# Graph attention with residual and norm: 35 more tiles of x kept in DRAM, and another order in the lead-in

## The chip, the cores and the metric

The kernel runs on one core of one Trainium2 chip. The metric is the device time of one execution in microseconds (us). TensorE (PE), VectorE (DVE), ScalarE (ACT) and GpSimd (POOL) compute; SyncE (SP), ACT and POOL issue DMA transfers. PEld stands for TensorE's loads of weights.

## The reference

For 16 graphs x of 1024 nodes with 512 features, all with the same 0/1 matrix adj of 1024 x 1024, attention with 8 heads of 64 is computed in which a node attends to its neighbours alone; a residual and a layer norm follow.

```python
q = x @ Wq + bq;  k = x @ Wk + bk;  v = x @ Wv + bv        # 8 heads of 64
scores = q . k / sqrt(64) + (1 - adj) * -1e9
out = softmax(scores) @ v @ Wo + bo
x = layernorm(x + out)                                      # over the 512 features, eps 1e-5
```

The inputs have few edges: the probability of an edge falls with both node numbers, so most nodes have at most eight neighbours and a few have many.

## The kernel before, in words

**Sparse attention by lists.** Nodes are ranked by their number of neighbours and put into eight tiles of 128, t = 0 to 7 (ADJ, `most`, `ranks`). A node of tile t has OWN[t] neighbours of its own (2, 1, 2, 3, 4, 5, 5, 7). What is above that in tiles 6 and 7 is spread over BLOCKS[t] further blocks (1 and 5), and a product with a 0/1 matrix, `sums`, adds these up. The lists of tiles 6 and 7 are made by `edges(6)` and `edges(7)`, two generators that search rows of adj (DVE maxima), place the result by a product with `before` (`poff`), write place marks (the lines at L677 to L688), multiply once more (`pe`), read out the keys (L702 to L714) and transpose the marks into `sums` (`pof`, copied by ACT).

**Blocks and steps.** For each batch b and tile t, a block is one neighbour for each of 128 nodes: POOL gathers 128 rows of k and v (`kvg`, L1260), DVE multiplies with q (`qk`, L1281) and sums by head (`s`, L1285), ACT takes the exponential and weighs v (`pv`, L1309), DVE adds up (L1325). There are 530 blocks. The program is written out by one loop over steps n, one block a step, with 39 steps ahead of block 0 (n = -39 to -1), the lead-in. Within a step, functions planned earlier by `later` run, then matmuls by an account of credit (`share`), then one piece of each generator in `preps` up to its next `yield`. Gathers run eight blocks ahead, products four steps ahead. The order on each engine is the order of the program; the engines wait for each other by semaphores.

**Dense work.** `fronts` is a list of matmul units for all batches: transpositions of x (`pxT`), then pairs of row tiles: q by plain products (`pq`), k and v by a Strassen-like form with seven products (`x`, `pp` for p4, p6 and p7, and `z`), evacuated by DVE and ACT (`e`, `w`, `g`, `kv`). Rows of q, k and v go to DRAM by SP. `finish` multiplies by Wo (`po`), and `complete` adds residual and bias and normalises; POOL scatters the rows to the output. Most PSUM results take one of four buffers with the tag "fill" (`fill_psum`); `x`, `z` and `sum` have their own.

**x for the residual.** x is gathered by rank twice by POOL: once for the dense work (`gather_x`, L1001) and once for the residual (`load_y`, L1029), unless the tile's number 8 b + t is in STORED. A stored tile is written by SP to `residual` out of its transposition step and read back by SP (L1026). The x tiles have three buffers; the gather that follows in the same buffer comes two steps later for a stored tile:

```python
if b * NT + t in STORED:
    nc.sync.dma_start(residual[b * NT + t], xs)
    later(2, lambda: load_x(n // NT, n % NT))
else:
    load_x(n // NT, n % NT)
```

**The lead-in around the change.** `edges(7)` starts at step -24 and `edges(6)` at -9 (REST_FROM). `bias_setup` starts at -8 (BIAS_AT): a broadcast of bk, norms of bk and bq (L399 to L405), transpositions of the biases (`pb`, L408 and L409), copies (L411 to L415, the last makes `bvb`), a product with Wo (`pb3`, L419; the trace calls both pb) and its addition to `bo_bc` (L421). `more_ranks` computes `shifts` and `others` at -7 and -6 on DVE (L552 to L578).

Of the kernel before, what the change touches and what calls it, by code (L numbers as in the profile page):

```python
# [10 lines left out]
F32 = mybir.dt.float32  # L11
# [20 lines left out]
KG_BUFS, Q_BUFS, QT_BUFS, PV_BUFS, Y_BUFS = 8, 5, 3, 5, 6  # L32
# [10 lines left out]
LAZY = 2  # L43

SPILL = (*(8 * b + t for b in range(4, 12) for t in (3, 6)), 102, 103, 106, 107)
STORED = {*SPILL, *(i for i in range(102, 128) if i % 8 > 1)}
LATE = 12

AHEAD_LAST = 11
# [24 lines left out]
P = 128  # L74
# [103 lines left out]
def kernel(  # L178
# [36 lines left out]
    nc = tc.nc  # L215
    B, N, D = x.shape
    HD = D // HEADS
    NPAIR = D // P
# [20 lines left out]
    ident = const.tile([P, P], F32, name="ident")  # L239
# [4 lines left out]
    bias_qk = const.tile([P, 2 * NPAIR], F32, name="bias_qk")  # L244
# [3 lines left out]
    def broadcast(t, v):  # L248
        nc.scalar.dma_start(t, bass.AP(tensor=v.tensor, offset=v.offset, ap=[[0, P], [1, D]]))
# [4 lines left out]
    with ExitStack() as main:  # L254
        one = main.enter_context(tc.tile_pool(name="one", bufs=1))
        work = main.enter_context(tc.tile_pool(name="work", bufs=1))
# [4 lines left out]
        def fill_psum(name):  # L261
            return psum.tile([P, HALF], F32, tag="fill", name=name, bufs=4)
# [80 lines left out]
        def number(b, t):  # L343
            return b * NT + t if t < NT else -1
# [4 lines left out]
        spill = {i: dram.tile([P, D], F32, name=f"spill_{i}") for i in SPILL}  # L349
        residual = {i: dram.tile([P, D], F32, name=f"residual_{i}") for i in sorted(STORED)}  # L350
        zeros = work.tile([P, D + HEADS], F32, tag="pv0", name="zeros", bufs=3)
        nc.gpsimd.memset(zeros, 0.0)
        bias_rows = work.tile([2 * NPAIR, D + HEADS], F32, tag="pv0", name="bias_rows", bufs=3)[:, 0:P]
        bv_rows = work.tile([NPAIR, D + HEADS], F32, tag="pv0", name="bv_rows", bufs=3)[:, 0:P]
# [37 lines left out]
            nc.scalar.dma_start(bv_rows, bv.rearrange("(c p) -> c p", p=P))  # L392

        def bias_setup():
            bk_bc = work.tile([P, D], F32, tag="y", name="bk_bc", bufs=Y_BUFS)
            broadcast(bk_bc, bk)
            yield
            n4 = small.tile([P, NPAIR], F32, name="bk_norms", bufs=1)
            nc.vector.tensor_tensor(bk_bc, bk_bc, bk_bc, op=OP.mult)  # L399
            nc.vector.tensor_reduce(n4, bk_bc.rearrange("p (h d) -> p h d", d=P), axis=AX.X, op=OP.add)  # L400
            nc.vector.tensor_reduce(bk_norm, n4, axis=AX.X, op=OP.max)
            n8 = small.tile([P, HEADS], F32, name="bq_norms", bufs=1)
            nc.vector.tensor_tensor(bk_bc, bq_bc, bq_bc, op=OP.mult)
            nc.vector.tensor_reduce(n8, bk_bc.rearrange("p (h d) -> p h d", d=HD), axis=AX.X, op=OP.add)
            nc.vector.tensor_reduce(bq_norm, n8, axis=AX.X, op=OP.max)  # L405
            yield
            pb = fill_psum("pb")
            nc.tensor.transpose(pb[:, 0:2 * NPAIR], bias_rows, ident[:2 * NPAIR, :2 * NPAIR])  # L408
            nc.tensor.transpose(pb[:, 2 * NPAIR:3 * NPAIR], bv_rows, ident[:NPAIR, :NPAIR])  # L409
            yield  # L410
            nc.vector.tensor_copy(bias_qk, pb[:, 0:2 * NPAIR])  # L411
            bv_col = one.tile([P, NPAIR], F32, name="bv_col")
            nc.vector.tensor_copy(bv_col, pb[:, 2 * NPAIR:3 * NPAIR])
            bvb = work.tile([P, NPAIR, P], F32, tag="y", name="bvb", bufs=Y_BUFS)
            nc.vector.tensor_copy(bvb, bv_col[:, :, None].to_broadcast([P, NPAIR, P]))  # L415
            yield
            pb = fill_psum("pb3")
            for c in range(NPAIR):
                nc.tensor.matmul(pb, bvb[:, c, :], W["o"][:, c, :], start=(c == 0), stop=(c == NPAIR - 1))  # L419
            yield  # L420
            nc.vector.tensor_tensor(bo_bc, pb, bo_bc, op=OP.add)  # L421
# [209 lines left out]
        def edges(t):  # L631
            nb, J, K = BLOCKS[t], DEGREE[t], OWN[t]
            tag, bufs = ("kvg", KG_BUFS) if J > 16 else ("kv", 5)
# [36 lines left out]
                nc.vector.tensor_tensor(check[:, 2 * NT + 1:2 * NT + 2], ranked[:, t, 1:2], st[:, 0:1], op=OP.subtract)  # L670

            nc.vector.tensor_scalar(deg, ranked[:, t, 1:2], -float(K), 0.0, op0=OP.add, op1=OP.max)
            yield
            po = fill_psum(f"poff_{t}")
            nc.tensor.matmul(po[:, 0:1], before, deg, start=True, stop=True)
            yield
            nc.vector.tensor_copy(off, po[:, 0:1])  # L677
            nc.vector.tensor_scalar(kl[:, J:J + 1], po[:, 0:1], -float(K), None, op0=OP.add)
# [7 lines left out]
            o, span = of, place[:, 0:nb * P]  # L686
            nc.vector.tensor_scalar(o, span, off, None, op0=OP.is_gt)
            nc.vector.scalar_tensor_tensor(o, span, end, o, op0=OP.is_le, op1=OP.mult)  # L688
            yield
            step = min(nb, HALF // (J + 3))  # L690
            assert step * J <= D
            for i0 in range(0, nb, step):
# [50 lines left out]
        def transpose_x(b, t):  # L743
            def pe():
# [5 lines left out]
                def out():  # L750
# [3 lines left out]
                    if t == 0 and b >= PAIRED_FROM:  # L754
# [7 lines left out]
                        nc.scalar.activation(sq[0:LONE, :], xs[0:LONE, :], AF.Square, accum_out=x_norm[0:LONE, b:b + 1])  # L762
                    if b * NT + t in STORED:
                        nc.sync.dma_start(residual[b * NT + t], xs)
# [251 lines left out]
        def load_y(b, t, k=None):  # L1016
# [7 lines left out]
            loaded[b, t] = now[0]  # L1024
            if number(b, t) in STORED:
                nc.sync.dma_start(Y[b, t], residual[b * NT + t])  # L1026
# [445 lines left out]
        for t, n in REST_FROM.items():  # L1472
            prep.setdefault(n, []).append(edges(t))
        prep.setdefault(BIAS_AT, []).append(bias_setup())
        prep.setdefault(CHECKS_AT, []).append(checks())
        preps = [loads(), ranks()]
# [146 lines left out]
```

## Time and profile before

| what | value |
|---|---|
| median of 3 runs | 1878.04 us (1875.33 to 1880.48) |
| profiled execution | 1888.5 us |
| its span, first to last instruction | 1886.7 us |
| mean granted TensorE clock | 0.988 |
| busy: PE, DVE, ACT, POOL | 1814.2, 1687.8, 1565.7, 1264.1 us |
| DMA | 544.64 MB, mean 289 GB/s |
| gathers of y by POOL | 93, mean 1096 ns each |
| stores and loads of `residual` by SP | 36 and 36, 256 KB each |

The profile is one execution; its rows are compared with its own span. Busy times of different engines overlap. In rows that show operations, an arrow points from what is read to what is written, with buffer numbers left out; a wait is given as engine, line, and what ended it.

### The profile page before, as it was taken

The page shows a single profiled execution, that of the slowest core. Times are in us where ns is not written, and L with a number is a line of the kernel's source. Part 1 is how long each engine was busy: PE and PEld are TensorE (multiplying, and loading weights), DVE is VectorE, ACT ScalarE, POOL GpSimd, SP SyncE. Part 2 cuts the span into 40 slices and gives each one's busy share as a digit, 9 for nine tenths or more (in the row PEclk, how much of TensorE's full clock was granted, in tenths as well). Part 3 has the DMA queues.
Part 4 walks back from the last instruction along what each step waited for, and adds up shares of the span by engine and source line. Part 5 has one row for each costly group of instructions (what it writes and reads, how often), then busy time and mean ns, then how long its engine had stood idle before and what let it go on. Part 6 is the DMA issues. An engine that isn't in the chain of part 4 may idle for free.

```text
span 1886.7 us, 25241 instructions
## 1 busy us (share of the span) xinstructions
PE 1814.2 (96%) x5136; PEld 878.0 (47%) x5150; DVE 1687.8 (89%) x3462; ACT 1565.7 (83%) x6184; POOL 1264.1 (67%) x1189
## 2 busy tenths in 40 slices
PE   7979999999999999999999999999999999999995
PEld 3434444454444444444444444444544444444442
DVE  6888788999988999999899999999999999997885
ACT  3627768988888897999889898999799999987785
POOL 1366665777675776767676776677767767665784
PEclk9989999999999999999999999999999999999997
DMA  7356687898888898998898988888988999899982
GB/s 280 115 167 213 214 271 244 281 338 294 310 278 268 288 315 308 310 319 305 286 310 304 328 291 322 312 297 319 316 322 306 312 352 337 297 329 316 350 312 110
DMA packets 188150, 544.64 MB, mean 289 GB/s; under 512 B 32602, under 2 KB 32622, under 8 KB 187986
## 3 DMA queue, kind: packets, MB, share of 16 engines
q0 software_dynamic: 116400, 382.82, 60.5%
q1 hardware_dynamic: 68510, 154.30, 22.0%
q10 hardware_dynamic: 3076, 5.82, 0.9%
q14 instruction: 121, 0.99, 0.2%
q8 instruction: 43, 0.70, 0.1%
HBM read 419.52 MB, written 144.34 MB: 299 GB/s over the span
## 4 chain that ended last, share of the span: by engine, by line
PE 64%; DVE 12%; ACT 9%; issue 5%; DMA 2%; POOL 2%; SPq 0%; another core or an unknown queue 0%; POOLq 0%; DVEq 0%; ACTq 0%
PE po L790 16%; PE pq L790 13%; PE pp L947 11%; PE x L947 8%; PE z L947 8%; ACT pv L1309 6%; PE poT L1369 2%; DVE qk L1281 2%; PE pxT L748 2%; DVE s L1285 2%; PE sum L1335 2%; PE sum L1334 2%; ACT sq_k L800 1%; DVE pv L1325 1%; POOL kvg L1260 1%
## 5 line engine op out<-in xcount | busy, mean ns | idle before, releaser
L1309 ACT ACTIVATE pv<-kvg,pv 128x64 f32<-128x64 f32 x3600 | 908.3, 342 | 0.9 <-issue 0.7
L1260 POOL DMA_INDIRECT kvg<-kv_pair,place_row x462 | 521.7, 1129 | 261.5 <-issue 89.6
L790 PE MATMUL po<-wo,oT 128*128 128x512 f32 x816 | 374.4, 596 | 0.8 <-DVE g L966 0.3
L790 PE MATMUL pq<-wq,xT 128*128 128x512 f32 x792 | 368.7, 596 | 1.3 <-DVE q L821 0.9
L1285 DVE TENSOR_REDUCE s<-qk 128x8 f32<-128x512 f32 x530 | 360.5, 680 | 6.7
L1281 DVE TENSOR_TENSOR qk<-qt,kvg 128x512 f32<-128x512 f32 x434 | 296.7, 684 | 0.0
L947 PE MATMUL x<-b,xT 128*128 128x512 f32 x504 | 238.9, 596 | 0.5 <-issue 0.4
L947 PE MATMUL pp<-t,s 128*128 128x512 f32 x504 | 237.2, 593 | 1.6 <-DVE t L383 1.6
L790 PEld LDWEIGHTS po<-wo,oT 128*128 128x128 f32 x816 | 154.1, 191 | 176.2 <-issue 167.0
L1325 DVE TENSOR_TENSOR pv<-pv,pv 128x520 f32<-128x520 f32 x329 | 228.5, 694 | 4.5 <-ACT pv L1309 2.6
L790 PEld LDWEIGHTS pq<-wq,xT 128*128 128x128 f32 x792 | 148.0, 191 | 165.7 <-issue 154.2
L1001 POOL DMA_INDIRECT x<-in_x_dram,asked_row x120 | 130.3, 1086 | 85.2 <-PE pxT L748 34.6
L1125 POOL DMA_INDIRECT out_dram<-y,asked_row x129 | 148.3, 1150 | 39.2 <-issue 25.1
L1296 ACT ACTIVATE pv<-s,absent 128x8 f32<-128x8 f32 x434 | 127.5, 295 | 49.6 <-DVE s L1285 38.6
L800 ACT ACTIVATE sq_k<-kv 128x128 bf16<-128x128 f32 x512 | 151.1, 302 | 12.0 <-ACT sq_k L800 3.9
L947 PEld LDWEIGHTS x<-b,xT 128*128 128x128 f32 x504 | 94.8, 192 | 109.4 <-issue 102.0
L947 PEld LDWEIGHTS pp<-t,s 128*128 128x128 f32 x504 | 94.0, 190 | 109.3 <-issue 101.3
L1214 POOL DMA_INDIRECT qg<-q_rows,query_row x96 | 109.9, 1145 | 27.9 <-issue 25.2
L947 PE MATMUL z<-b,s 128*128 128x512 f32 x252 | 121.9, 607 | 4.3 <-DVE kv L975 3.3
L1029 POOL DMA_INDIRECT y<-in_x_dram,asked_row x93 | 102.0, 1096 | 35.8 <-issue 26.8
L947 PE MATMUL pp<-t,xT 128*128 128x512 f32 x252 | 120.4, 601 | 4.6 <-ACT mean L862 4.1
L1121 ACT ACTIVATE y<-y,stats 128x512 f32<-128x512 f32 (+1 forms) x129 | 103.8, 807 | 17.9 <-DVE stats L1116 14.4
(276 smaller groups left out, 2759.6 us busy)
## 6 DMA issues: line engine op xcount, KB each, us to landing
kv_pair<-kv SPq DMA_DIRECT2D x98, 512.0 KB
q_rows<-q SPq DMA_DIRECT2D x106, 256.0 KB
qt<-q_rows SPq DMA_DIRECT2D x98, 256.0 KB
residual<-x SPq DMA_DIRECT2D x36, 256.0 KB
y<-residual SPq DMA_DIRECT2D x36, 256.0 KB
kv_rows<-kv SPq DMA_DIRECT2D x15, 512.0 KB
kvg<-kv_pair,place_row POOLq DMA_INDIRECT x462
kv_pair<-kv SPq DMA_DIRECT2D x28, 256.0 KB
```

The source lines that it names most:

```text
L790: nc.tensor.matmul(p, lhs(c), w[:, c, :], start=(c == 0), stop=(c == NPAIR - 1))
L800: nc.scalar.activation(sq, s[:, ts(h, P)], AF.Square, scale=scale, accum_out=sums[:, h:h + 1])
L947: nc.tensor.matmul(R[bank], l[:, ts(c, P)], right[:, c, :], start=(first and c == 0), stop=(c == 1), skip_group_check=True,)
L1001: nc.gpsimd.indirect_dma_start(out=y, out_offset=None, in_=x_rows, in_offset=bass.IndirectOffsetOnAxis(ap=asked_row[:, t:t + 1], axis=0), ...
L1125: nc.gpsimd.indirect_dma_start(out=out_rows[b, t], out_offset=bass.IndirectOffsetOnAxis(ap=rows, axis=0), in_=y, in_offset=None, element_o ...
L1214: nc.gpsimd.indirect_dma_start(out=q, out_offset=None, in_=q_rows[b % ROWS], in_offset=bass.IndirectOffsetOnAxis(ap=rows, axis=0))
L1260: nc.gpsimd.indirect_dma_start(out=KG[n], out_offset=None, in_=rows, in_offset=bass.IndirectOffsetOnAxis(ap=(place_row if b else key_row)[ ...
L1281: nc.vector.tensor_tensor(QK[n], q, KG[n][:, 0:D], op=OP.mult)
L1285: nc.vector.tensor_reduce(S[n], QK.pop(n).rearrange("p (h d) -> p h d", d=HD), axis=AX.X, op=OP.add)
L1296: nc.scalar.activation(PV[n][:, D:], S.pop(n), AF.Exp, bias=bias)
L1309: nc.scalar.activation(pv[:, ts(h, HD)], v[:, ds(D + h * HD, HD)], AF.Copy, scale=pv[:, D + h:D + h + 1])
L1325: nc.vector.tensor_tensor(PV[b, t], PV[b, t], pv, op=OP.add)
```

## The change

Three edits are made. First, STORED takes in the tiles with numbers from 10 to 101 whose t is 2, 5 or 7: 35 tiles, 71 in all. Second, in `bias_setup` the transpositions of the biases come first, their copies one step later and ahead of the norms, and the product with Wo comes four yields behind the norms. Third, in `edges` there are four yields instead of one ahead of the first product, two instead of one behind it, and three instead of one behind the place marks.

```diff
-STORED = {*SPILL, *(i for i in range(102, 128) if i % 8 > 1)}
+STORED = {*SPILL, *(i for i in range(10, 102) if i % 8 in (2, 5, 7)), *(i for i in range(102, 128) if i % 8 > 1)}
...
         def bias_setup():
+            pb = fill_psum("pb")
+            nc.tensor.transpose(pb[:, 0:2 * NPAIR], bias_rows, ident[:2 * NPAIR, :2 * NPAIR])
+            nc.tensor.transpose(pb[:, 2 * NPAIR:3 * NPAIR], bv_rows, ident[:NPAIR, :NPAIR])
             bk_bc = work.tile([P, D], F32, tag="y", name="bk_bc", bufs=Y_BUFS)
             broadcast(bk_bc, bk)
+            yield
+            nc.vector.tensor_copy(bias_qk, pb[:, 0:2 * NPAIR])
+            bv_col = one.tile([P, NPAIR], F32, name="bv_col")
+            nc.vector.tensor_copy(bv_col, pb[:, 2 * NPAIR:3 * NPAIR])
+            bvb = work.tile([P, NPAIR, P], F32, tag="y", name="bvb", bufs=Y_BUFS)
+            nc.vector.tensor_copy(bvb, bv_col[:, :, None].to_broadcast([P, NPAIR, P]))
             yield
             n4 = small.tile([P, NPAIR], F32, name="bk_norms", bufs=1)
...
             nc.vector.tensor_reduce(bq_norm, n8, axis=AX.X, op=OP.max)
-            yield
-            pb = fill_psum("pb")
-            nc.tensor.transpose(pb[:, 0:2 * NPAIR], bias_rows, ident[:2 * NPAIR, :2 * NPAIR])
-            nc.tensor.transpose(pb[:, 2 * NPAIR:3 * NPAIR], bv_rows, ident[:NPAIR, :NPAIR])
-            yield
-            nc.vector.tensor_copy(bias_qk, pb[:, 0:2 * NPAIR])
-            bv_col = one.tile([P, NPAIR], F32, name="bv_col")
-            nc.vector.tensor_copy(bv_col, pb[:, 2 * NPAIR:3 * NPAIR])
-            bvb = work.tile([P, NPAIR, P], F32, tag="y", name="bvb", bufs=Y_BUFS)
-            nc.vector.tensor_copy(bvb, bv_col[:, :, None].to_broadcast([P, NPAIR, P]))
-            yield
+            for _ in range(4):
+                yield
             pb = fill_psum("pb3")
...
             nc.vector.tensor_scalar(deg, ranked[:, t, 1:2], -float(K), 0.0, op0=OP.add, op1=OP.max)
-            yield
+            for _ in range(4):
+                yield
             po = fill_psum(f"poff_{t}")
             nc.tensor.matmul(po[:, 0:1], before, deg, start=True, stop=True)
             yield
+            yield
             nc.vector.tensor_copy(off, po[:, 0:1])
...
             nc.vector.scalar_tensor_tensor(o, span, end, o, op0=OP.is_le, op1=OP.mult)
-            yield
+            for _ in range(3):
+                yield
             step = min(nb, HALF // (J + 3))
```

## The prediction

> **What bounds the kernel now.** I read the busy shares and the slices of the page first, then the windows by stage, then TensorE's waits, then the instructions in order of time where it waits.
>
> ```profile
> PE 1814.2 (96%) x5136; PEld 878.0 (47%) x5150; DVE 1687.8 (89%) x3462; ACT 1565.7 (83%) x6184; POOL 1264.1 (67%) x1189
> ...
> PE   7979999999999999999999999999999999999995
> ...
> q0 software_dynamic: 116400, 382.82, 60.5%
> q1 hardware_dynamic: 68510, 154.30, 22.0%
> ```
>
> TensorE (PE) is busy for all but 72.5 us of the span (1886.7 - 1814.2). The low slices stand at both ends. By the windows, PE is busy 1430.5 of the 1450 us from 250 to 1700: 19.5 us of idle. Up to 250 us it idles 27.1 us, and 10.1 from 50 us on are in this window:
>
> ```profile
> 100.00:150.00 50.00, 38.94 (x104) 17.44 (x103) 38.66 (x112) 15.12 (x62) 28.87 (x27) 0.86 0.57 181
> 150.00:200.00 50.00, 49.86 (x144) 23.90 (x143) 42.32 (x85) 40.15 (x172) 33.58 (x32) 1.00 0.66 211
> ```
>
> The columns are the stretch, then busy us of PE, PEld, DVE, ACT and POOL, granted clock, DMA share, GB/s. TensorE's waits there are two (us in total, times, longest):
>
> ```profile
> PE pb L419 <- DVE bv_col L413: 8.9, 1, 8.9
> PE poff L675 <- DVE check L670: 2.1, 1, 2.1
> ```
>
> These are the instructions around the first (start, us, what, idle before):
>
> ```profile
> 127.12 1.88 PE L790 MATMUL pq<-wq,xT 128*128 128x512 f32 x4
> 137.94 6.43 PE L419 MATMUL pb<-wo,bvb 128*128 128x512 f32 x8 [8.94 <-DVE bv_col L413]
> ...
> 152.40 3.60 PE L790 MATMUL pq<-wq,xT 128*128 128x512 f32 x8
> ```
>
> The bias product (pb3 in the code, pb in the trace) waits 8.94 us for a copy that VectorE (DVE) reaches late, and its eight matmuls then take 6.43 us where eight others take 3.60: 2.8 us more at a low clock. The prize is 8.9 + 2.8 = 11.7 us. DVE in the same place:
>
> ```profile
> 115.82 0.69 DVE L966 TENSOR_TENSOR g<-pp,w 128x512 f32<-128x512 f32 x1 [2.71 <-PE pp L947]
> ...
> 137.27 0.15 DVE L413 COPY bv_col<-pb 128x4 f32<-128x4 f32 x1
> ...
> 139.12 0.68 DVE L963 TENSOR_TENSOR w<-pp,e 128x512 f32<-128x512 f32 x1
> ...
> 146.47 0.68 DVE L821 SCALAR_TENSOR_TENSOR q<-pq,bq_bc 128x512 f32<-128x512 f32 x1
> ```
>
> From 117 to 142 DVE has no gap but short ones between its own dependent instructions. So here two engines are near their limit: PE waits for one copy, but behind that copy DVE is full.
>
> **What the Trainium skill says.** "TensorE: Matmul & The Clock Gate", Part 1, has the array fall to half clock after some 3.4 us idle and come back after as long a busy stretch; the 6.43 against 3.60 us agrees. The same page's table calls VectorE's queue strictly in order, so a copy emitted behind other work waits for all of it: that is the stall above. "DMA: Bandwidth & Descriptors", Issuing engines are not separate DMA queues: transfers of SP and of GpSimd (POOL) share 16 DMA engines, so a move from one to the other saves issue time and no transfer; the two queue rows agree in that both draw on one share. The same page's Anatomy of one DMA prices a transfer at 2.0 us + bytes/436 GB/s, 2.6 us for 256 KB as an estimate; the trace has no landing times for it, but its longest wait for such a store, 3.1 us, is near.
>
> **Part 1: 35 tiles kept.** Tiles 10 to 101 with t of 2, 5, 7: 33 in batches 1 to 11 and two in batch 12. Each adds a store of x and a load of y on SP (70 issues at the 0.41 us of the present rows, 29 us on an engine that mostly waits), and takes a gather of y from POOL: 35 x (1.10 + 0.30 issue) = 49 us of POOL. 35 gathers of x come two steps later (some 7 us; a step is about 3.3 us, 1737 us over 530 steps). They are used about 8 steps on (60 pairs over some 520 steps), so no transposition comes to wait.
>
> DMA: 70 x 256 KB = 18.4 MB more on q1 at 22.0/154.3 % per MB is +2.6 % of the span; 9.2 MB fewer on q0 at 60.5/382.8 is -1.5 %. The share goes up by 1.2 points, from 0.90 to about 0.92 in the middle. It is 0.95 at 1450 to 1500 us and PE is busy for all 50.0 us there.
>
> What could that change on the path? TensorE's longest waits from 250 to 1700 us:
>
> ```profile
> PE pm L858 <- DVE vsum L854: 3.8, 3, 1.9
> PE z L947 <- DVE kv L975: 3.3, 1, 3.3
> PE poT L1369 <- DVE o L1355: 3.0, 1, 3.0
> ```
>
> and POOL's for the stores of today:
>
> ```profile
> POOL x L1001 <- DMA residual<-x: 7.4, 5, 3.1
> ```
>
> No row names POOL or a transfer, so POOL's 49 us are hidden behind PE and gain nothing on the path. A gather of x that waits for its store holds the gathers of keys behind it in POOL's queue, for which DVE would wait; at 7.4/36 us each that is 7 us in all, at the longest each time 35 x 3.1 = 108. DVE waited for one such gather for 2.7 us in the whole stretch, so their lead of up to eight steps covers the first and probably most of the second. On SP a load of y waits for an older output store (13.7 us in 4 of 36 cases); the k, v and q stores and loads of query tiles queue behind it, and have steps to spare. I take 0, between -4 (a fifth of the 19.5 us idle) and +6 (a few late gathers).
>
> **Part 2: the lead-in.** Step numbers follow from the starts in the code; the trace has the same order. TensorE's instructions for list 7 move from steps -12, -10, -9 and -8 to -9, -4, -3 and -2 (a product, five products, four transpositions and one); DVE's nine small ones for its places (L677 to L688, 2.1 us) from -11 to -7 and nine behind the second product (L702 to L714, 3.0 us) from -9 to -3. ACT's two copies of sums go six steps later too. List 6's go from -3, -2, -1, 0 to 0, 2, 5, 6. The two bias transpositions go from -6 to -8, the three copies (0.6 us) from -5 to -7, the norms (3.0 us) from -7 to -6, the product from -4 to -2 and the addition from -3 to -1. The broadcast of bk stays at its step on ACT's queue.
>
> The 2.1 us wait of poff goes, and is worth nothing: the next thing on PE is the product of means at 109.66, which starts as DVE ends its sums at 109.6. From there I count on.
>
> PE: the second pp product of the pair (p7) ends at 115.7 as before, then z, p4, the second z and x, p6 and half of pq without the lists' products: 127.2. List 7's product, the other half of pq, the next x and the list's transpositions: 132.2. Then p7 of the next pair needs one of the four PSUM buffers "fill". They hold p6 (freed by w on DVE), pq (by q), and list 7's two results. Today the slot of p6 is free at 139.8 and nobody waits, since PE itself stands until 137.9.
>
> DVE: it loses the work that filled its gaps. It now idles from 111 to 115.8 and, behind g, from 116.4 to 118.5 for z. Then: second z, sums for the next pair and p4, to 121.2; places of list 7, to 123.2; shifts (2.1), to 125.3; copies, 125.9; one evacuation and the chain of others (L569 to L578, 4.7), 131.3; codes of list 6 (1.1), 132.4; norms, 135.5; sum and maxima (3.1), 138.5; first qk and s (1.3), 139.8; w to 140.4. So p7 starts at 140.4 and PE has stood for 8.2 us: **the stall is moved and not removed**, its releaser now w. List 7's nine come at -3: DVE is at 145.9 then, and list 7's last transposition and the bias product wait for those slots until about 146.2. At a low clock the product ends at 152.6, at the full one at 149.7.
>
> Before, PE was through the same work (p7 of step -2) at 149.6. That is 0 to +3 us. List 6's work (2.8 us of DVE) no longer stands ahead of step 1, but ahead of steps 3 and 7, where DVE is still full (to 165), so it mostly comes back. If the 3.7 us that DVE loses between its own instructions L569 to L578 fall away, w is ready at 136.7 and the result is -3. From 166 to 218 us PE has no wait, so what it has at 165 is passed on. I take +1, ends -12 (the prize) and +8 (below).
>
> **Sum.** 0 + 1 = +1 us against the profiled execution of 1888.5 us (span 1886.7 and 1.8 around it). The median of the runs is 1878.0, 10.5 us lower; the difference is carried over as it is: 1879.
>
> **Rivals.** *The stall really goes* (faster). DVE's order lets PE run on, p7 finds a slot in time, and the 8.9 + 2.8 us are kept: 1878 - 12 = 1866. For it: PE has no other wait from 94 to 165 us. Against: DVE has no gap until 142. Part 1 giving 4 us as well would make 1862.
>
> *DVE becomes the bound of the lead-in* (slower). Its idle from 109 to 151 us, 6.0 today (2.7, 0.4, 2.1 and 0.8), becomes 6.9 ahead of step -7, plus up to 4.5 while the addition at step -1 waits for a product at low clock: +5.4, and list 6's 2.8 us in full steps make +8: 1886. The point from which it decides: w later than 139.8, and the product still at low clock. For it: the count above has 140.4. Against: work moved behind step 6 may find a gap.
>
> *Gathers come late* (slower) by SP's and POOL's queues, from some 20 us of lag in POOL: 10 late ones at 2.7 us would be +27, 1905. Nothing in the trace comes near, and I give it little. *The change doesn't do what it says*: y has only one reader of the list of kept tiles, and x is stored from it; I leave this at 2 in 100, inside no change.
>
> **How the numbers follow.** A measurement of this kernel tells some 0.3%, 5.6 us, from no change. Stall moved, within that: 0.41. Stall gone: 0.33. DVE bound or late gathers: 0.26. The range leaves out the last 1 in 10 on each side: from 1863, the prize with part of part 1's gain, to 1890, the second rival with half of part 1's loss; the likeliest case alone would be 1873 to 1884.
>
> **What would show it.** Right: PE's wait for bv_col gone and in its place a wait of some 8 us of pp for w near step -4; the first key products of batch 0 on DVE near 138.6; y from POOL in 58 gathers and 71 each of store and load; no new wait on DMA in the middle. Wrong: PE without a wait between 127 and 150 us; DVE or PE waiting for kvg; or the middle shorter by more than 4 us.

## The result and the profile after

The change made the kernel a little faster: 1877.69 us (1867.63 to 1882.87) against 1880.72 us (1875.33 to 1886.42), 22 runs each on one chip. These two medians are 3.0 us apart; the ratio on record, which is not that of the medians, is 0.9975, with a 95% interval of 0.9964 to 0.9987, so 4.7 us. Ratios below are of this kind. The forecast was 1879.0 with no change as the likeliest case.

The two profiled executions exaggerate this: that of before took 1888.5 us, above all its 22 timed runs, that of after 1867.63, the lowest of its 22. From these two profiles an order of events can be read, and no sum of 20 us explained.

The page of after, with the rows that answer to those of before (PE and its slices, the two queues of GpSimd's gathers and of SP):

```profile
PE 1812.4 (97%) x5150; PEld 879.3 (47%) x5150; DVE 1686.2 (90%) x3462; ACT 1564.6 (84%) x6184; POOL 1237.3 (66%) x1154
...
PE   7989999999999999999999999999999999999995
...
q0 software_dynamic: 113600, 373.64, 59.1%
q1 hardware_dynamic: 78590, 172.65, 24.8%
```

POOL has 35 instructions fewer and 26.8 us less of busy time (35 x 1.10 = 38.5 were forecast); q0 fell and q1 rose by the forecast bytes (-9.2 and +18.4 MB), and their shares add to 83.9% of a shorter span where they were 82.5%. For the lead-in, the three fences that follow show one window by stage (us of PE, PEld, DVE, ACT and POOL, clock, DMA share, GB/s), PE's waits from 94 to 260 us, and PE's instructions in order of time:

```profile
100.00:150.00 50.00, 40.99 (x105) 18.43 (x104) 38.15 (x104) 20.47 (x88) 29.25 (x28) 0.83 0.63 201
```

```profile
PE pp L950 <- DVE w L966: 4.5, 1, 4.5
PE pm L861 <- DVE vsum L857: 3.0, 1, 3.0
PE pq L793 <- DVE y L1102: 1.8, 1, 1.8
PE pof L722 <- DVE query_row L717: 1.5, 1, 1.5
```

```profile
136.35 3.78 PE L950 MATMUL pp<-t,s 128*128 128x512 f32 x4 [4.49 <-DVE w L966]
141.59 0.45 PE L722 MATMUL pof<-ident,codes 128*128 128x128 f32 x1 [1.46 <-DVE query_row L717]
142.05 6.49 PE L419 MATMUL pb<-wo,bvb 128*128 128x512 f32 x8
```

The wait for `bv_col` (8.9 us) and that of poff (2.1) are gone; in their place stand waits of 4.5, 3.0 and 1.5 us on DVE. The bias product follows at low clock again, 6.49 us for eight matmuls. At its end, at 148.4 us, after is 1.2 us ahead of before (149.6). Outside the lead-in the waits on transfers that touch the change, from 250 to 1700 us, are small and few:

```profile
POOL kvg L1263 <- ACT pv L1312: 96.0, 66, 5.3
...
POOL x L1004 <- DMA residual<-x: 6.7, 5, 1.8
DVE qk L1284 <- DMA kvg<-kv_pair,place_row: 6.2, 5, 3.1
```

The first row was shorter before:

```profile
POOL kvg L1260 <- ACT pv L1309: 65.3, 47, 6.2
```

POOL now waits longer for `kvg` buffers, that is, it has more time in hand.

### The profile page after: what moved, and what is told of

It reads as the page before. It is cut to its first block, busy times and chain, and to the rows that moved or that the text cites. A ratio compares the mean times of both kernels' runs of the same rounds, so it can differ in the third digit from the quotient of the medians.

```text
span 1865.9 us, 25322 instructions
## 1 busy us (share of the span) xinstructions
PE 1812.4 (97%) x5150; PEld 879.3 (47%) x5150; DVE 1686.2 (90%) x3462; ACT 1564.6 (84%) x6184; POOL 1237.3 (66%) x1154
## 4 chain that ended last, share of the span: by engine, by line
PE 67%; DVE 11%; ACT 7%; DMA 5%; issue 4%; POOL 1%; SPq 0%; POOLq 0%; DVEq 0%; ACTq 0%
PE po L793 16%; PE pq L793 13%; PE pp L950 12%; PE x L950 8%; PE z L950 8%; ACT pv L1312 4%; PE poT L1372 2%; PE pxT L751 2%; DVE qk L1284 2%; PE sum L1338 2%; DVE s L1288 2%; PE sum L1337 2%; DMA oTs<-spill 1%; ACT sq_k L803 1%; DMA kvg<-kv_pair,place_row 1%
## 5 line engine op out<-in xcount | busy, mean ns | idle before, releaser
L1263 POOL DMA_INDIRECT kvg<-kv_pair,place_row x462 | 535.6, 1159 | 285.7 <-ACT pv L1312 85.8
L1217 POOL DMA_INDIRECT qg<-q_rows,query_row x96 | 106.9, 1114 | 26.8 <-issue 25.7
L950 PE MATMUL z<-t,s 128*128 128x512 f32 x252 | 118.6, 593 | 0.0
L950 PE MATMUL pp<-t,xT 128*128 128x512 f32 x252 | 118.5, 592 | 0.0
```

Of the source, the lines that this page charges most:

```text
L950: nc.tensor.matmul(R[bank], l[:, ts(c, P)], right[:, c, :], start=(first and c == 0), stop=(c == 1), skip_group_check=True,)
L1217: nc.gpsimd.indirect_dma_start(out=q, out_offset=None, in_=q_rows[b % ROWS], in_offset=bass.IndirectOffsetOnAxis(ap=rows, axis=0))
L1263: nc.gpsimd.indirect_dma_start(out=KG[n], out_offset=None, in_=rows, in_offset=bass.IndirectOffsetOnAxis(ap=(place_row if b else key_row)[ ...
```

## The experiments

They ran on five chips, B to F; the chip of the result above is called A, and the record doesn't say whether it is a sixth. The kernel before was run on each beside them, and every ratio below is to that. Each chip was used in one session, so that "chip" below always means a chip in its session.

| chip | before, median of runs | kernels and ratios |
|---|---|---|
| A | 1880.7 of 22 | whole change 0.9975 |
| B | 1862.9 of 51 | stored tiles 0.9989, lead-in 1.001, bias copies 0.9997, lists 1.001 |
| C | 1893.8 of 53 | whole change 0.9956, bias copies with stored tiles 0.9954, 54 stored 0.9952 |
| D | 1882.0 of 67 | stored tiles 0.9958, small gather 0.9994, later only 0.999, unread stores 0.9995 |
| E | 1862.7 of 43 | stored tiles 1.0007, powers 1.0001, added gathers 1.0002, lead-in 1.001 |
| F | 1863.4 of 25 | powers 1.0003, added gathers 1.000 |

**The parts, on chip B.** My theory was that the lead-in had given the gain; the rival, that the stored tiles had.

The stored tiles alone:

```diff
-STORED = {*SPILL, *(i for i in range(102, 128) if i % 8 > 1)}
+STORED = {*SPILL, *(i for i in range(10, 102) if i % 8 in (2, 5, 7)), *(i for i in range(102, 128) if i % 8 > 1)}
```

> Part 1 alone: the 35 further tiles of x are kept, the lead-in is as before. My theory (the lead-in gives the gain, through ACT, which weighs block 0 at 139.5 us instead of 148.3 and so is not late with the copy of means at 222): the same as before within 2 us, and the TensorE wait of 8.9 us for bv_col is there. Rival A (the relief of POOL and the later gathers of x give it): 4 to 5 us faster, and PE's idle time from 250 to 1700 us falls from 19.5 to some 14 us. Rival B (the gain is in both in equal parts): 2 to 3 us faster.

0.9989 (0.9979 to 0.9998): 2 us faster. The lead-in alone is the rest of the change, with STORED as before:

> Part 2 alone: the lead-in of the changed kernel, STORED as before. My theory: 4 to 5 us faster; PE waits some 4.5 us for w and no more for the copy of means near 215 us, and has its x of batch 2 (after the first pm of batch 1) some 7 us earlier than before. Rival A: the same as before within 2 us, since the stall is only moved. Rival B: 2 to 3 us faster.

1.001 (1.0001 to 1.002): 1.9 us slower. My theory fell. The bias copies alone are the edit in `bias_setup` without that in `edges`, the lists alone the reverse:

> The bias half of part 2 alone: transpositions and copies ahead of the norms, the product at step -2; the lists of tiles 6 and 7 as before. If the stall at bv_col is what counts: PE has no wait of over 2 us between 115 and 150 us, since list 7's results are out of the PSUM buffers early, and the kernel is 4 to 8 us faster. If the work order of DVE is the limit (the prediction's count): PE's wait goes over to w or q on DVE, 2 to 6 us of it, and the time is within 3 us of before.

0.9997 (0.9987 to 1.0007).

> The lists half of part 2 alone: products of lists 6 and 7 later, bias as before. By the prediction's count: the 2.1 us wait of poff goes over to the sums of v, PE stands at bv_col at least as long as before (9 us), now perhaps also for a PSUM buffer, and the time is 0 to 4 us more than before. If the lists' delay is what gives the gain: 2 to 5 us faster.

1.001 (1.0003 to 1.0018). The later lists are what costs. In the four profiles PE's longest wait in the lead-in is 7.5 us in two pieces with the bias copies alone (for `est`, which the list's place work delays), 6.6 with the lists alone (for `bvb`), 4.5 with both, 5.3 with neither: each order has its own. Together the parts come to 0.9999 here, while the whole gave 0.9975 on chip A: either they act together, or the chip matters.

**The whole and larger doses, on chip C.** The first is the changed kernel again.

> The whole change once more. Adding up: the stored tiles alone gave a ratio of 0.9989 and the lead-in alone 1.001, so if the parts add up the whole is at 0.9999 (within 0.001), about 0.2 us under the kernel before. Working together: if the stored tiles pay only with the later lists, or the other way round, the ratio is again near 0.9975, some 4.7 us under the kernel before, and below both parts alone.

0.9956 (0.993 to 0.9982): a gain again, and not 0.9999. That it is larger than on chip A is not shown, as the intervals overlap. Next, STORED with every t > 1 of tiles 10 to 101, lead-in as before:

```diff
-STORED = {*SPILL, *(i for i in range(102, 128) if i % 8 > 1)}
+STORED = {*SPILL, *(i for i in range(10, 102) if i % 8 > 1), *(i for i in range(102, 128) if i % 8 > 1)}
```

> Stored tiles alone, lead-in as before, and a larger dose: every tile with t > 1 of tiles 10 to 101 is stored, 54 more than before in place of 35 (90 in all). If each gather taken from GpSimd pays, the gain of 0.9989 grows with the dose to 0.9983 (3.2 us). If only the first ones pay, it stays at 0.9989. If SP's stores and loads hold up its queue or the DMA engines, it is eaten up: 1.000 or more.

0.9952 (0.9931 to 0.9973). Then the stored tiles with the bias copies, lists as before:

> Stored tiles and the bias copies ahead of the norms, with the lists' products where they were before: the change without the part that cost time alone (1.001). If the parts add up: 0.9989 times 0.9997, so 0.9986, 2.6 us under the kernel before and below the whole change. If the stored tiles need the later lists, it is no better than 1.000 and above the whole change.

0.9954 (0.9934 to 0.9974). All three hold the 35 tiles and cannot be told apart: no gain of 54 tiles over 35 can be seen, and no effect of the later lists. The kernel before, for its profile:

> The kernel before, unchanged, for a profile of it beside those of the parts on one chip. If the wait of ScalarE at 215 to 222 us and the late product of means of batch 1 at 229 us in the first profile belong to the kernel, they are seen again and the product starts over 8 us later than in the kernel with the whole change; if they were that one execution's, the product of means of batch 1 starts within 2 us of where it does in the parts (210 to 212 us) and the lead-in alone shows no gain in its markers.

It took 1891.5 us. The waits of ScalarE at 215 to 222 us and of PE's pp for `mean` (4.1 us at 222.8 in the first profile) are not there, so they were that one execution's. The expectation also took a mark wrongly: the product of means of batch 1 starts at 214.9 us in the first profile, not at 229, and here at 214.5; with the whole change on this chip it starts at 221.4, with the bias copies and stored tiles at 212.4. So single executions on this chip scatter by more at this place than the lead-in could give.

**What in the stored tiles gains, on chip D.** The stored tiles alone as the measure:

> The 35 stored tiles alone, lead-in as before, on another chip, as the measure for the three that follow. The gain was 0.9989 where the kernel before took 1862.9 us, and with either lead-in 0.9954 to 0.9956 where it took 1893.8 us. If the gain goes with the chip's own time, it lies between these, and nearer to 0.9955 the longer the kernel before takes.

0.9958 (0.9941 to 0.9975), 7.9 us. In what follows MORE is the set of the 35 tiles. Where a diff below doesn't say otherwise, STORED takes them in; in the kernels with only the later gather of x and with added gathers it doesn't. A small gather in the place of each dropped one, its result unread:

```diff
                 nc.sync.dma_start(Y[b, t], residual[b * NT + t])
+                if number(b, t) in MORE:
+                    idle = small.tile([P, 1], F32, tag="idle", name=f"idle_{b}_{t}", bufs=4)
+                    nc.gpsimd.indirect_dma_start(
+                        out=idle, out_offset=None, in_=place_of,
+                        in_offset=bass.IndirectOffsetOnAxis(ap=key_row[:, 0:1], axis=0), bounds_check=N, oob_is_err=False,
+                    )
```

> As the stored tiles alone, but GpSimd still issues a gather in the place of each of the 35 dropped ones: one number for each partition from a small table into a scratch tile that nobody reads, about 1.0 us of GpSimd as before, and hardly any bytes. If the gain comes from GpSimd's time, it is gone: 1.000 of before. If it comes from the dropped bytes of the gather's queue, or from where the x gathers and the stores stand, the time is that of the stored tiles alone.

0.9994 (0.9977 to 1.001): most of the gain is gone, and nothing of it is left that could be seen. Against the stored tiles on the same chip the ratio of medians is 1.0030 (1.0006 to 1.0047, by resampling the 22 runs of each). A small gather takes POOL as long as a large one (1144 and 1069 ns on average in this profile). Only the later gather of x:

```diff
-                    if b * NT + t in STORED:
-                        nc.sync.dma_start(residual[b * NT + t], xs)
+                    if b * NT + t in STORED | MORE:
+                        if b * NT + t in STORED:
+                            nc.sync.dma_start(residual[b * NT + t], xs)
                         later(2, lambda: load_x(n // NT, n % NT))
```

> The kernel before, with nothing more stored: only the gathers of x that follow the 35 tiles go out two places later, as the stored tiles' code has them. If the gain comes from that place in GpSimd's queue, the time is that of the stored tiles alone. If it comes from fewer gathers, 1.000 of before.

0.999 (0.9972 to 1.0009). The stores too, with the residual gathered as before:

```diff
-            if number(b, t) in STORED:
+            if number(b, t) in STORED - MORE:
                 nc.sync.dma_start(Y[b, t], residual[b * NT + t])
```

> The 35 tiles are stored by SP, but the residual is still gathered by GpSimd, and the stored copies are read by nobody. It has the cost of the stores (35 times 256 KB of DMA work, 35 more places in SP's queue) and the later gathers of x, without the relief of GpSimd. If the stores cost what the relief hides, it is slower than before: 1.001 to 1.002. If they are free, it is at the time of the kernel with the later gathers of x alone.

0.9995 (0.997 to 1.0019). So neither the place of x's gathers nor the stores nor, for the most part, the 256 KB of each gather make the gain: it is GpSimd's gather as an issued operation, its time on GpSimd or its entries in the software queue.

**Time or queue, on chips E and F.** The powers replace the small gather by work without DMA:

```diff
                 nc.sync.dma_start(Y[b, t], residual[b * NT + t])
+                if number(b, t) in MORE:
+                    idle = small.tile([P, 1], F32, tag="idle", name=f"idle_{b}_{t}", bufs=4)
+                    for _ in range(2):
+                        nc.gpsimd.tensor_tensor(idle, mean, neg_half, op=OP.pow)
```

Two powers take 1.47 us (734 ns each in the profile), somewhat more than a gather. The added gathers put the small gather ahead of each of the 35 gathers of the kernel before.

> The 35 stored tiles alone, as the measure on this chip for the three that follow. So far: 0.9989 where the kernel before took 1862.9 us, 0.9958 where it took 1882.0 us. If the gain goes with the chip's own time it is near 0.999 on a chip of some 1863 us and near 0.996 on one of 1880 us or more.

1.0007 (0.9997 to 1.0016): no gain on this chip, as there was nearly none on chip B.

> As the stored tiles alone, and in the place of each of the 35 dropped gathers GpSimd computes two powers of one column into a scratch tile that nobody reads (0.6 us each by the powers of the norms in the profiles, so about the time of a gather, 1.1 us) and issues no DMA. If the gain is GpSimd's time, it is gone: 0.999 to 1.000 of before. If it is the gather as a DMA (its descriptors, its place in the software queue), the time is that of the stored tiles alone.

1.0001 (0.9989 to 1.0013).

> The kernel before, with 35 small gathers of one number for each partition added ahead of the 35 gathers of the residual: GpSimd's time of the dose in the other direction (35 times 1.1 us and 0.3 us of issue, 49 us in all). If GpSimd's time counts as the stored tiles suggest, it is slower by about what they gain: 1.004 on a chip of 1880 us, 1.001 on one of 1863 us. If GpSimd has slack for it, 1.000.

1.0002 (0.9993 to 1.0012).

> The lead-in's changes alone once more. They gave 1.001 (1.0001 to 1.002) on the one chip on which they were timed alone; the whole change against the bias copies with the stored tiles gave no difference on another (0.9956 and 0.9954). If they cost 1 to 2 us by the waits in the lead-in, 1.0005 to 1.001 again; if they are worth something where the stored tiles gain more, under 1.000.

1.001 (1.0001 to 1.002): the lead-in's cost came out the same on a second chip. As there was no gain here to take away, powers and added gathers were run once more; the chip, F, was again one of that kind:

> The stored tiles alone with two computed powers on GpSimd in the place of each dropped gather, once more, for the last chip (1862.7 us for the kernel before) showed no gain of the stored tiles to take away. On a chip where the kernel before takes 1880 us or more, the stored tiles gave 0.9954 to 0.9958: if the gain is GpSimd's time this is at 0.998 to 1.000, if it is the gather's descriptors and its place in the software queue, at 0.996. On a chip of some 1863 us: 1.000 in both cases, and nothing is told apart.

1.0003 (0.9993 to 1.0013).

> The kernel before with 35 small gathers added, once more. On a chip where the kernel before takes 1880 us or more: 1.004 if 35 gathers count for as much when they are added as when they are taken away, 1.000 if only taking them away counts. On a chip of some 1863 us: 1.000 as on the last one (1.0002).

1.000 (0.999 to 1.001). On these two chips 35 gathers of GpSimd's time count for nothing that could be seen, in either direction. Time or queue on chips A, C and D stays open.

**Where the chips differ.** The profiles divide into two kinds. These are rows of ScalarE's waits from 250 to 1700 us with the stored tiles alone on chip D, in which "issue" is a wait for nothing that the profile shows, and "remote" one whose releaser it doesn't find:

```profile
ACT e L960 <- remote: 8.6, 1, 8.6
ACT e L960 <- issue: 8.3, 7, 4.4
ACT kv L826 <- issue: 6.3, 7, 3.2
```

For the same kernel on chip E there is no such row; the longest in the same view are all waits for PE or DVE:

```profile
ACT e L960 <- PE x L947: 43.9, 27, 5.1
ACT pv L1296 <- DVE s L1285: 40.6, 34, 3.2
ACT kv L826 <- PE x L947: 31.2, 25, 4.0
```

Added up over DVE and ACT, rows of these two names hold 26 to 69 us in each of the ten profiles of chips A, C and D, and nothing in each of the ten of B, E and F. One such pause, on DVE, with the later gathers of x alone on chip D:

```profile
1320.71 0.68 DVE L1283 TENSOR_TENSOR qk<-qg,kvg 128x512 f32<-128x512 f32 x1
1321.30 0.69 DVE L1327 TENSOR_TENSOR pv<-pv,pv 128x520 f32<-128x520 f32 x1
1321.91 0.68 DVE L1287 TENSOR_REDUCE s<-qk 128x8 f32<-128x512 f32 x1
1329.58 0.69 DVE L1101 TENSOR_TENSOR y<-po,y 128x512 f32<-128x512 f32 x1 [6.99 <-PE pp L949]
```

DVE stands for 7 us; PE is named, but the product that y reads had ended at 1321.4 and PE went on without it. ACT stutters in the same 10 us (waits "issue" of 0.4 to 0.8 us between its instructions, then one of 2.6). Then PE ran out of work and stood for 4 us.

This pause was seen once. Many others come back at the same place of the program: DVE's kv, between 577 and 590 us, waits 1.90 us in eight of the ten profiles, and ACT's e, between 829 and 845 us, 3.1 us in six, in both cases on all three chips. The gain of the stored tiles was seen alone on D and with either lead-in on C, where 54 tiles alone gave as much; on A it is an estimate (below). On the chips without pauses it is 2 us or nothing.

POOL's spare time moved as its gathers did, on every chip. Its waits for `kvg` to be released by ACT or DVE, from 250 to 1700 us:

| chips | none stored in addition | 35 stored | small gather or powers in their place | 54 stored |
|---|---|---|---|---|
| with pauses (A, C, D) | 184, 186, 188, 194 | 218, 225, 228, 229 | 179 | 256 |
| without (B, E, F) | 200, 200, 202, 203 | 239, 251 | 185, 191 | not run |

(The first column holds the kernels that gather all 93 residual tiles, whatever their lead-in and stores; with 35 small gathers added it is 158 and 165.) On chips with pauses the kernels at 218 us and above have the gain, and those below don't. A likely reading is that after a pause POOL is behind, and with some 40 us more in hand it has the next gathers out sooner. That chain was not followed in a trace: it is argued, not shown. The pauses themselves are not fewer with the stored tiles: their rows add up to 42.5 us with them on chip D, and to 42.6, 44.0 and 26.3 in the three kernels there without the gain.

Where the gain falls is seen on chip D alone. From the second product of means to the last it takes 1493.7 us with the stored tiles and 1498.4 to 1499.9 in the other three. On chip C the same stretch takes 1503.0 to 1503.7 us in the three kernels with the gain and 1502.5 in the one profile of before: there, single executions hide it.

## Why the prediction was wrong, and where it was right

**Part 1, taken at 0: the step that failed.** The sentence was that no row names POOL or a transfer, "so POOL's 49 us are hidden behind PE and gain nothing on the path". That nearly holds on chips B and E (-2.0 and +1.3 us by the ratios). On D it is worth 7.9 us, twice the end of -4 that I had left open; on C the three kernels with it gave 8 to 9. On A it was not timed alone: -4.7 for the whole and +1.9 for the lead-in, as timed on B and E, leave -6.6 as an estimate. The small gathers show the term: 35 issued gathers. Why they cost time where no wait names them stays open. That DVE almost never waited for a gather was read rightly; that a queue's lag costs nothing as long as no wait names it was the error. The profile of before had rows of the other kind, and I passed over them:

```profile
ACT e L960 <- remote: 8.8, 2, 5.8
```

The prediction had named a middle shorter by more than 4 us as a sign of being wrong; on D it came, with 5 to 6 us.

The terms that were feared came out at nothing: no loss showed from the stores and the two steps' delay of x (0.9995 and 0.999, each within its interval of 1), POOL's waits for a store of x were 6.7 us over 71 stores where 7.4 over 36 had suggested twice as much, DVE's waits for gathers rose by 5.4 us in all (2.7 to 8.1) and the share of the DMA by 1.4 points (1.2 forecast; of the 1.4 some 0.9 come from the shorter span, 82.5 x 1886.7/1865.9 = 83.4).

**Part 2, taken at +1: near, and in part by luck.** Measured alone it is +1.9 us, twice. The mechanism is the forecast one: the wait for bv_col gives way to a wait of p7 for w. That wait was 4.5 and not 8.2 us. In the sum, the chain of L569 to L578 had 4.7 us as in the profile of before; it took 1.3, from 125.8 to 127.1, its own gaps having gone, as the text allowed for. These are w and the first key product, earlier than the forecast 139.8 and 138.5:

```profile
134.30 0.68 DVE L1284 TENSOR_TENSOR qk<-qt,kvg 128x512 f32<-128x512 f32 x1
135.02 0.69 DVE L1288 TENSOR_REDUCE s<-qk 128x8 f32<-128x512 f32 x1
135.62 0.68 DVE L966 TENSOR_TENSOR w<-pp,e 128x512 f32<-128x512 f32 x1
```

The gaps in that chain were read as the kernel's own, but they come and go with the execution. Two of them in the profile of before, and the wait for the bias copies with the same lead-in on chip B:

```profile
131.51 0.16 DVE L577 SCALAR_TENSOR_TENSOR key_row<-absent,others 128x2 int32<-128x2 f32 x1 [1.14 <-DVE absent L576]
132.92 0.17 DVE L578 TENSOR_SCALAR absent<-absent 128x2 f32<-128x2 f32 x1 [1.25 <-DVE key_row L577]
```

```profile
PE pb L419 <- DVE bvb L415: 5.3, 1, 5.3
```

In all ten profiles of chips B, E and F the chain takes 1.3 to 1.6 us, on A, C and D 2.8 to 6.1 in five of ten. In the six profiles of B, E and F with the old lead-in the stall is 5.2 to 6.6 us. So 2.3 to 3.7 of the 8.9 us that the change aimed at were not the kernel's. The count had these gaps on both sides of its difference, so they fell out of it; its branch without them, -3, took them from one side only. That +1 came near to +1.9 is luck to that extent.

The low clock of the bias product isn't fixed either: with the lead-in alone its eight matmuls took 5.40 us on B and 3.70 on E, close to the 3.60 that eight take at full clock.

The lead of 1.2 us at 148.4 us is then no gain of the new order, since only before had those gaps. From the first product of means to the transpositions behind p7 and the bias product it takes 34.9 to 36.5 us in the six profiles on chips B, E and F with the old lead-in, and 36.8 and 38.0 in the two with the new one alone. To the second product of means it takes 100.4 to 101.8 us in the six, 102.0 and 103.1 in the two, 102.2 with the lists alone and 99.7 with the bias copies alone. So the loss is there at the end of the stall already; list 6's later work, which the sum expected to cost, isn't needed to explain it.

One reading of the prediction is off without any effect: the window from 100 to 150 us has 11.1 us of idle PE (50.00 - 38.94), not 10.1.

**The rivals.** That the stall really goes did not happen: PE's waits there became several shorter ones. VectorE did not become the bound by 8 us, and the gathers were not late. That the sum was close (1879.0 and 1877.7) says little, for what gain there is came from the part that was priced at nothing.

## What to carry to other kernels

A queue that no wait names can still be worth relieving. Here it was where profiles had rows without a known releaser; that spare time on the queue absorbs such pauses is the likely reason, not a shown one. Look for such rows before pricing a relief at zero, and don't carry a gain of half a per cent over from one chip to another without timing it there. Look at a stall in a second execution before you count it as the prize: of the 8.9 us here 5.2 to 6.6 came back in other executions. In a lead-in where the engine behind the stall is full, a new order only renames the stall.

## What the runs showed of the hardware

**Chips, or sessions, differ by more than the change.** The same kernel before had medians of 1862.7, 1862.9 and 1863.4 us on chips E, B and F and 1880.7, 1882.0 and 1893.8 on A, D and C, and only the latter have the pauses. Whether it goes with the chip or with the session on it was not tested. What a pause is was not settled. Some of DVE's longer ones have a transfer of the instruction queue near their start, but such transfers come about every 11 us, so that says little.

**A short wait of TensorE can cost twice.** On chips B, E and F the product z waits 2.4 us for kv near 557 us, whatever the lead-in. Here it is in two executions of the lead-in alone, on chip B and on chip E:

```profile
558.22 3.42 PE L950 MATMUL z<-b,s 128*128 128x512 f32 x4 [2.38 <-DVE kv L978]
```

```profile
560.35 1.98 PE L950 MATMUL z<-b,s 128*128 128x512 f32 x4 [2.38 <-DVE kv L978]
```

After the same wait the four matmuls took 3.42 us in the one and 1.98 in the other; over the ten profiles of these chips they range from 1.98 to 3.68. In the first the record of the clock has one half-speed stretch of 3.4 us (a mean clock of 0.70 from 557 to 561 us and 0.87 from 561 to 565), in the second none there, and the batch around it takes 120.2 and 118.5 us: 1.7 us for a wait of 2.4. The Trainium skill, "TensorE: Matmul & The Clock Gate", Part 1, has the clock judged in free-running windows of some 3.4 us, which agrees with the length and with the luck of it, but asks for at least one idle window; here a wait of 2.38 us by the profile was enough. A profile of one execution can differ from the next by this alone.
